# Block sums of a symmetrised matrix in four instructions, and the held groups' stores on SyncE

## The chip, the core and the metric

The kernel runs on one core of a Trainium2 chip. The metric is the device time of one execution in microseconds (us), lower being better; a time given for a kernel is the median over several runs. The profile is of one execution. The engines are TensorE (PE, with its weight loads as PEld), VectorE (DVE), ScalarE (ACT), GpSimd (POOL) and SyncE (SP); SP, ACT and POOL issue the DMA transfers.

## The reference

```python
def reference(x, adj, L0_gnn_W):          # x (8, 4096, 256), adj (4096, 4096), W (256, 256), float32
    HW = jnp.einsum('bnf,fo->bno', x, W)
    A_norm = jax.nn.relu((adj + adj.T) * 0.5)
    D = jnp.sum(A_norm, axis=1)
    d_inv_sqrt = jnp.where(D > 0, jnp.where(D > 0, D, 1.0) ** (-0.5), 0.0)
    DAD = d_inv_sqrt[:, None] * A_norm * d_inv_sqrt[None, :]
    out = relu(jnp.einsum('nm,bmo->bno', jnp.eye(4096) - DAD, HW))
    return _layernorm(x + out, axis=-1)
```

`adj` is sparse, and denser in its first rows and columns: entry (i, j) is set with a probability that falls with i and j.

## The kernel before

The work has two phases. The **first phase** (to about 595 us of the profile) goes over the upper triangle of `adj` in blocks of 512 x 512: row `i` from 0 to 7, column `j` from `i` to 7. For a pair of blocks (i, j) and (j, i) it loads both (`load_adj`, L411, by SyncE, four buffers), transposes one with TensorE in 16 pieces (`symmetrise`, L421), adds the other from SBUF with VectorE, 512 columns at a time (L425), and so makes two blocks `sym` (three buffers). `keep` then applies ReLU and the factor 0.5 with ScalarE (L429), sums every 64 columns into `part` with VectorE (L430), and stores the block to `a_dram` by a DMA that ScalarE issues (L436). The four transposed strips of a block need one PSUM bank each; four banks (`b0`) turn round between these, the transposes of x and the products with W, so TensorE can go on only as VectorE and ScalarE empty them.

Beside the blocks TensorE makes the products with W, one group of 128 rows (all eight batches) at a time (`form`): it transposes x (L519), ScalarE copies the result (L520), TensorE multiplies by W (L530). The result `g` has to be scaled by the row's degree root `r`. For rows whose degrees are known ScalarE scales it out of PSUM (L540) and stores it to `g_dram` (L545). The last ten groups, 22 to 31, are made early and **held** in SBUF (L542). When a row `i` of blocks is through, `degrees(i)` sums `part` (L447), makes `e` (L449), takes the root with GpSimd (L450) and its negative (L451). `release` then scales the held groups of that row, the odd ones with VectorE (L553), the even ones with ScalarE (L555), and stores them to `g_dram` (L556). `lower_diagonal` corrects the diagonal blocks (L459, stored by L462). Groups 22 and 23 belong to row 5, groups 24 to 27 to row 6, groups 28 to 31 to row 7. After its store each group is multiplied with a strip of A (`multiply`, L488, into the banks `lead`), which makes the first 128 rows of the output.

From row 2 on VectorE also builds lists of which pieces of A are not empty (`patterns`, `place`, `place_rest`, `spread`, `index`, L199 to L384), from the sums in `part`.

The **second phase** gathers those pieces of A and the rows of g by indirect DMAs that GpSimd issues (L806, L819; 12 buffers for g), multiplies them (L1008), and finishes each 128 rows with ReLU, residual and layer norm on ScalarE and VectorE; SyncE stores the output (L729). The gathers read `g_dram`, so the first one waits for the last held group's store.

The instructions of an engine run in the order of its list. A scheduler makes that list from the program and from its own costs of instructions, so an edit can move other instructions; pools of buffers and semaphores do the rest. A DMA waits on its issuing engine for what it stores, and everything behind it on that engine waits with it.

Of the kernel before, what the change touches and what calls it, by code (L numbers as in the profile page):

```python
# [11 lines left out]
ALU = mybir.AluOpType  # L12
AX = mybir.AxisListType
# [46 lines left out]
def kernel(  # L60
# [25 lines left out]
    nc = tc.nc  # L86
    B, N, F = x.shape
    FO = w.shape[1]
    P = 128
    S = 512  # L90
    A = S // P
# [5 lines left out]
    Q = 64  # L97
# [17 lines left out]
    part = const.tile([P, NB, N // Q], F32, name="part")  # L115
# [8 lines left out]
    g_dram = dram.tile([N + 1, G], F32, name="g_dram")  # L124
# [270 lines left out]
    with (  # L395
# [31 lines left out]

        def keep(i, j, sym, diag):
            nc.scalar.activation(sym, sym, AF.Relu, scale=0.5)  # L429
            nc.vector.tensor_reduce(  # L430
                part[:, i * A : (i + 1) * A, j * S // Q : (j + 1) * S // Q],
                sym.rearrange("p a (c q) -> p a c q", q=Q),
                AX.X,
                ALU.add,
            )
            nc.scalar.dma_start(  # L436
                a_dram[i * S : (i + 1) * S, j * S : (j + 1) * S].rearrange("(a p) s -> p a s", p=P), sym
            )
            if i == j:
                for a in range(A):  # L440
                    nc.gpsimd.tensor_copy(diag[:, a, :], sym[:, a, a * P : (a + 1) * P])
# [38 lines left out]
        def fetch(m):  # L480

            t = strips.tile([P, P], F32, tag="strip", name=f"strip_{m}")
            load(t, a_dram[m * P : (m + 1) * P, :P])
            return t
# [65 lines left out]
        def release(m):  # L550
            g = held.pop(m)
            if m % 2:
                nc.vector.tensor_scalar(g, g, r[:, m : m + 1], None, ALU.mult)  # L553
            else:
                nc.scalar.mul(g, g, r[:, m : m + 1])  # L555
            nc.scalar.dma_start(g_dram[m * P : (m + 1) * P, :], g)  # L556
            waiting.append((m, g, fetch(m)))

        diags = {}
# [1 line left out]
        def release_all(i):  # L561
            for m in range(i * A, (i + 1) * A):
                if m in held:
                    release(m)
            lower_diagonal(i, diags.pop(i))
# [43 lines left out]
        for i in range(NS):  # L609
            diag = stat1.tile([P, A, P], F32, tag="diag", name=f"diag_{i}")  # L610
            for j in range(i, NS):
# [27 lines left out]
                for (rows, cols, _, _), sym in parts:  # L639
                    keep(rows, cols, sym, diag)  # L640
# [448 lines left out]
```

## Time and profile before

| | us |
|---|---|
| median of 6 runs (1526.8 to 1532.9) | 1530.88 |
| the profiled execution | 1528.14 |
| its span, first to last instruction | 1526.4 |

| engine | busy us | share of the span |
|---|---|---|
| PE | 1443.0 | 95% |
| PEld | 761.8 | 50% |
| DVE | 980.7 | 64% |
| ACT | 371.0 | 24% |
| POOL | 696.0 | 46% |

The groups that the diff touches: 64 sums L430 of 128x2048 elements, 145.5 us busy in all, 2280 ns each; ten stores L556 of 1024 KB, 9.5 us from issue to landing.

How to read it: lines of the timeline give the start and the length in us, engine, line and operation, and in brackets the idle time of the engine just before and what ended it. `L430` is line 430 of the kernel before; a tile's name stands as output<-input. A duration is that of one instruction from its start to its end; instructions that are queued on VectorE overlap a little, so the distance of their starts is shorter. The granted clock is 1.00 when TensorE runs at full speed. In the chain that ended last, each piece of time is put down to the instruction or transfer on which the next one waited.

### The profile page before, as it was taken

How to read it: one execution, taken by the hardware profiler on the slowest of the kernel's cores; microseconds unless marked ns; L12 is line 12 of the kernel's file. 1: busy time of each engine (PE TensorE's matmuls, PEld its weight loads, DVE VectorE, ACT ScalarE, POOL GpSimd, SP SyncE). 2: the span in 40 equal slices, each digit the busy share in tenths (PEclk: the TensorE clock that was granted, in tenths of full speed). 3: DMA queues.
4: the chain of work that ended last, by engine and by line, in shares of the span. 5: the costliest groups of instructions: out<-in, count | busy, mean ns of one | idle time of the engine just before them, and what ended most of it. 6: DMA issues, size and time to landing. Idle time of an engine off the chain costs nothing.

```text
span 1526.4 us, 19342 instructions
## 1 busy us (share of the span) xinstructions
PE 1443.0 (95%) x6440; PEld 761.8 (50%) x6440; DVE 980.7 (64%) x3013; ACT 371.0 (24%) x462; POOL 696.0 (46%) x1053
## 2 busy tenths in 40 slices
PE   5999989989989989999999999999999999999994
PEld 5877877767767764433333333333433333333331
DVE  4676578888646460464759669768046877898533
ACT  3655544535434450010100100100010011001111
POOL 3002010010303315766767666666655767666653
PEclk9999999989999999999999999999999999999997
DMA  9999999999979988999999999999989999999995
GB/s 334 370 371 401 395 380 361 360 369 349 344 250 363 335 345 354 419 417 409 381 398 389 384 408 370 401 389 383 394 306 398 345 388 404 401 396 371 381 397 183
DMA packets 216714, 564.50 MB, mean 370 GB/s; under 512 B 16550, under 2 KB 104918, under 8 KB 180134
## 3 DMA queue, kind: packets, MB, share of 16 engines
q0 software_dynamic: 54224, 304.94, 50.3%
q1 hardware_dynamic: 90352, 123.74, 23.3%
q10 hardware_dynamic: 72032, 134.51, 23.3%
q8 instruction: 54, 0.88, 0.2%
q14 instruction: 52, 0.43, 0.1%
HBM read 443.61 MB, written 136.34 MB: 380 GB/s over the span
## 4 chain that ended last, share of the span: by engine, by line
PE 69%; DMA 14%; DVE 9%; issue 5%; ACT 2%; POOL 2%; POOLq 0%; ACTq 0%; DVEq 0%
PE py L1008 48%; PE pg L530 9%; DMA g<-g_dram,gi 9%; PE lead L488 5%; DMA a_dram<-sym 3%; DVE sym L425 3%; PE xtr L519 3%; PE tr L421 3%; DVE part L430 2%; ACT sym L429 1%; DMA xin<-in_x_dram 1%; PE lists L356 1%; DMA ga<-a_dram,ai 1%; POOL limit L165 0%; POOL base L166 0%
## 5 line engine op out<-in xcount | busy, mean ns | idle before, releaser
L1008 PE MATMUL py<-g,ga 128*64 128x512 f32 (+1 forms) x2872 | 811.9, 597 | 14.7 <-DMA g<-g_dram,gi 12.3
L1008 PEld LDWEIGHTS py<-g,ga 128*64 128x64 f32 (+1 forms) x2872 | 290.9, 150 | 522.3 <-issue 498.6
L819 POOL DMA_INDIRECT g<-g_dram,gi x268 | 307.2, 1146 | 210.9 <-DMA g<-g_dram,gi 82.0
L806 POOL DMA_INDIRECT ga<-a_dram,ai x268 | 291.1, 1086 | 107.5 <-issue 68.3
L681 ACT ACTIVATE y<-py,minus_r 128x512 f32<-128x512 f32 x120 | 82.4, 687 | 806.4 <-PE py L1008 714.1
L692 DVE TENSOR_TENSOR xr<-xr,y 128x2048 f32<-128x2048 f32 x31 | 71.1, 2292 | 303.7 <-ACT y L681 249.3
L530 PE MATMUL pg<-w_sb,xt 128*128 128x256 f32 x1024 | 232.9, 386 | 5.2 <-ACT xt L520 5.2
L425 DVE TENSOR_TENSOR sym<-tr,adj 128x512 f32<-128x512 f32 x256 | 162.8, 683 | 95.6 <-PE tr L421 78.7
L530 PEld LDWEIGHTS pg<-w_sb,xt 128*128 128x128 f32 x1024 | 196.4, 195 | 33.4 <-ACT xt L520 5.6
L430 DVE TENSOR_REDUCE part<-sym 128x32 f32<-128x2048 f32 x64 | 145.5, 2280 | 61.7 <-ACT sym L429 61.7
L421 PE MATMUL tr<-ident,adj 128*128 128x128 f32 x1024 | 138.4, 285 | 31.6 <-DVE sym L425 20.0
L429 ACT ACTIVATE sym<-sym 128x2048 f32<-128x2048 f32 x64 | 122.6, 1916 | 130.9 <-DVE sym L425 118.4
L450 POOL TENSOR_TENSOR r<-e,neg_half 128x4 f32<-128x4 f32 x8 | 8.3, 1039 | 317.0 <-DVE e L449 234.7
L421 PEld LDWEIGHTS tr<-ident,adj 128*128 128x128 f32 x1024 | 118.8, 146 | 61.3 <-DVE sym L425 32.7
L697 DVE BATCH_NORM_STATS2 stats<-xr 128x6 f32<-128x256 f32 x256 | 87.2, 412 | 16.1 <-POOL xr L692 14.9
L519 PE MATMUL xtr<-ident,xin 128*128 128x128 f32 x512 | 72.4, 288 | 16.4 <-DVE sym L425 15.0
L721 DVE TENSOR_SCALAR xr<-xr,mv,root 128x256 f32<-128x256 f32 x248 | 83.6, 409 | 0.1
L488 PE MATMUL lead<-gt,strip 128*128 128x512 f32 x176 | 83.0, 598 | 0.0
L540 ACT ACTIVATE gt<-pg,r 128x512 f32<-128x512 f32 x88 | 60.6, 688 | 75.8 <-PE pg L530 71.9
L520 ACT COPY xt<-xtr 128x512 f32<-128x512 f32 x128 | 67.7, 591 | 45.7 <-PE xtr L519 45.1
L1008 PE MATMUL py<-g_hub,ga 128*128 128x512 f32 x176 | 78.3, 598 | 0.0
L335 DVE TENSOR_TENSOR hot<-iota_q,at 128x1024 bf16<-128x1024 f32 x64 | 74.3, 1221 | 2.8 <-DMA a_dram<-sym 2.8
(139 smaller groups left out, 812.2 us busy)
## 6 DMA issues: line engine op xcount, KB each, us to landing
adj<-in_adj_dram SPq DMA_DIRECT2D x64, 1024.0 KB, 10.6
a_dram<-sym ACTq DMA_DIRECT2D x64, 1024.0 KB, 9.3
xr<-in_x_dram ACTq DMA_DIRECT2D x32, 1024.0 KB, 26.3
out_dram<-xr SPq DMA_DIRECT2D x31, 1024.0 KB, 25.4
xin<-in_x_dram SPq DMA_DIRECT2D x44, 512.0 KB, 11.4
g_dram<-gt ACTq DMA_DIRECT2D x22, 1024.0 KB, 7.6
xin<-in_x_dram POOLq DMA_DIRECT2D x20, 512.0 KB, 7.2
g_dram<-held ACTq DMA_DIRECT2D x10, 1024.0 KB, 9.5
```

What stands on the lines that cost most here:

```text
L421: ins = nc.tensor.transpose(pt[:, c * P : (c + 1) * P], tji[:, c, a * P : (a + 1) * P], ident)
L425: nc.vector.tensor_add(sym[:, a, :], pt, tij[:, a, :])
L429: nc.scalar.activation(sym, sym, AF.Relu, scale=0.5)
L430: nc.vector.tensor_reduce(part[:, i * A : (i + 1) * A, j * S // Q : (j + 1) * S // Q], sym.rearrange("p a (c q) -> p a c q", q=Q), AX.X, A ...
L488: nc.tensor.matmul(lead[c], lhsT=strip, rhs=g[:, c * S : (c + 1) * S], start=not done, stop=len(done) == NB - 1, skip_group_check=True,)
L519: nc.tensor.transpose(pt[:, k, c, :], xin[b // H][:, b % H + k, c * P : (c + 1) * P], ident)
L530: ins = nc.tensor.matmul(pg[:, k * FO : (k + 1) * FO], lhsT=xt[:, b + k, c, :], rhs=w_sb[:, c, :], start=(c == 0), stop=(c == FC - 1),)
L697: nc.vector.bn_stats(stats[:, b, :], z[:, b, :])
L721: nc.vector.tensor_scalar(z[:, b, :], z[:, b, :], mv[:, b, 0:1], rstd[:, b : b + 1], ALU.subtract, ALU.mult,)
L806: nc.gpsimd.indirect_dma_start(out=at if both else at[:, :P], out_offset=None, in_=a_pairs if both else a_rows, in_offset=bass.IndirectOff ...
L819: nc.gpsimd.indirect_dma_start(out=gt, out_offset=None, in_=g_dram, in_offset=bass.IndirectOffsetOnAxis(ap=gi[:, t : t + 1], axis=0), boun ...
L1008: last_product = nc.tensor.matmul(py[2 * u + 1 + b][c][rows, :], lhsT=at[:, off + rows.start : off + rows.stop], rhs=gt[:, c * S : (c + 1) ...
```

## The change

The sums of 64 columns in `keep` are made by one instruction for each of the four 128-row parts of a block, not by one for the whole block: 256 instructions over 512 elements a partition in place of 64 over 2048. The stores of the ten held groups in `release` are issued by SyncE, not by ScalarE. On SyncE's list the stores of groups 22 and 23 stand ahead of the load of the last block (7, 7), and the other eight behind it, ahead of the first store of the output.

```diff
         def keep(i, j, sym, diag):
             nc.scalar.activation(sym, sym, AF.Relu, scale=0.5)
-            nc.vector.tensor_reduce(
-                part[:, i * A : (i + 1) * A, j * S // Q : (j + 1) * S // Q],
-                sym.rearrange("p a (c q) -> p a c q", q=Q),
-                AX.X,
-                ALU.add,
-            )
+
+            for a in range(A):
+                nc.vector.tensor_reduce(
+                    part[:, i * A + a, j * S // Q : (j + 1) * S // Q],
+                    sym[:, a].rearrange("p (c q) -> p c q", q=Q),
+                    AX.X,
+                    ALU.add,
+                )
             nc.scalar.dma_start(
                 a_dram[i * S : (i + 1) * S, j * S : (j + 1) * S].rearrange("(a p) s -> p a s", p=P), sym
             )
...
-            nc.scalar.dma_start(g_dram[m * P : (m + 1) * P, :], g)
+            nc.sync.dma_start(g_dram[m * P : (m + 1) * P, :], g)
             waiting.append((m, g, fetch(m)))
```

## The prediction

> **What bounds the kernel now.** I read the page first, then busy time by stage, then the chain of work that ended last, then the timelines of VectorE, TensorE and ScalarE where that chain leaves TensorE.
>
> ```profile
> span 1526.4 us, 19342 instructions
> PE 1443.0 (95%) x6440; PEld 761.8 (50%) x6440; DVE 980.7 (64%) x3013; ACT 371.0 (24%) x462; POOL 696.0 (46%) x1053
> ```
>
> TensorE is busy for 95% of the span, but both edits lie in the first 570 us. The stages differ (columns: length, then busy us and instructions of PE, PEld, DVE, ACT, POOL, the granted TensorE clock, the DMA share, GB/s):
>
> ```profile
> 40.00:220.00 180.00, 175.27 (x1018) 145.41 (x1018) 115.16 (x135) 101.71 (x128) 14.12 (x26) 1.00 1.04 382
> 220.00:360.00 140.00, 125.35 (x677) 97.59 (x676) 123.53 (x369) 63.13 (x73) 6.00 (x14) 0.95 0.99 360
> 360.00:560.00 200.00, 181.24 (x978) 141.25 (x977) 115.92 (x169) 94.25 (x109) 44.64 (x74) 0.95 0.88 327
> ```
>
> Up to 220 us the DMA engines are full (1.04). From 220 to 360 VectorE is busy 88%, and 98% from 240 to 280, since the index lists are placed there; TensorE loses 15 us. From 360 to 560 TensorE loses 19 us in gaps with single causes. From 564 on the chain is TensorE without a gap until 962, so what the first phase loses is carried to the end.
>
> **The price of one smaller sum.** The rows are the sum over a block and, nearest in size, the sum of 256 columns for the degrees.
>
> ```profile
> L430 DVE TENSOR_REDUCE part<-sym 128x32 f32<-128x2048 f32 x64 | 145.5, 2280 | 61.7 <-ACT sym L429 61.7
> L447 DVE TENSOR_REDUCE deg<-part 128x4 f32<-128x256 f32 x8 | 3.3, 417 | 0.1
> ```
>
> From start to start, with work queued behind, the large one takes 2.19 us (548.66 to 550.85) and the small one 0.32 (546.40 to 546.72). That is 1.04 ns an element and 0.05 us fixed, so 512 elements take 0.59 us; the 512-column adds of L425 follow each other at 0.60. Four make 2.39 us: 0.20 more per block, 64 x 0.20 = 12.8 us of VectorE in all. The bounds: nothing at all, or +0.45 if each shows the 0.68 us that an add lasts by itself minus a little overlap (4 x 0.66 = 2.64). I take 0.20, since the queued rows are the nearest.
>
> The Trainium skill, "VectorE: DVE Perf Modes", section on the TRN2 errata, speaks against this half: each instruction pays a fixed cost, so many small ones pay it many times. Its measured form for a single operation, (N+151)/0.96 ns, would give 4 x 0.69 - 2.29 = 0.47 a block, an estimate of 30 us in all; the queued starts 0.60 apart in this trace show that most of that fixed part overlaps.
>
> **Where 0.20 us reaches the end.** In 40 to 220 the chain contains five sums, but it also goes through stores of 11 us on full DMA engines: I take nothing, and 1.0 if that cover fails. Elsewhere the chain lists the sums in its own pieces:
> - 220 to 300: five, +1.0 us.
> - 320 to 360: four, +0.8.
> - The pair at 378.44, with TensorE idle 2.58 us for the add behind it: +0.4.
> - 448.0, 454.4 and 458.8: +0.6.
> - 515.08, in front of the degrees of row 5, whose root scales the group that TensorE waits 1.04 us for: +0.2.
>
> Together +3.0.
>
> **Two places where the order of VectorE changes.** The changed kernel's list of VectorE instructions is the old one, with quarters of sums slipped between small operations. Two of the moves matter. First, the diagonal block of row 3:
>
> ```profile
> 302.52 0.69 DVE L425 TENSOR_TENSOR sym<-tr,adj 128x512 f32<-128x512 f32 x1
> 303.12 0.17 DVE L326 CAST at<-digit 128x32 f32<-128x32 int32 x1
> 303.21 4.47 DVE L430 TENSOR_REDUCE part<-sym 128x32 f32<-128x2048 f32 x2
> ...
> 308.91 0.69 DVE L425 TENSOR_TENSOR sym<-tr,adj 128x512 f32<-128x512 f32 x1
> 310.08 0.17 DVE L451 TENSOR_SCALAR minus_r<-r 128x4 f32<-128x4 f32 x1 [0.48 <-POOL r L450]
> ...
> 310.36 1.21 DVE L459 SCALAR_TENSOR_TENSOR diag<-ident,minus_e,diag 128x128 f32<-128x128 f32 x4
> ```
> ```profile
> 308.91 1.97 PE L519 MATMUL xtr<-ident,xin 128*128 128x128 f32 x8 [4.99 <-DVE sym L425]
> 310.67 8.06 PE L530 MATMUL pg<-w_sb,xt 128*128 128x256 f32 x32
> ```
>
> Now the second add stands ahead of the pair of sums, the third and fourth behind it; TensorE waits 4.99 us for the PSUM banks they free. In the new list only the first add is ahead; the second and third come after the pair, and the fourth after `minus_r`, which waits for GpSimd's root, and the four L459. With the row's own steps: first add done 302.4, eight sums of 0.6 and a cast to 307.4, degrees and small ones 0.6, add 308.6, the next 309.35, the root 1.04 us after `e` so `minus_r` at 310.0, then 1.85 us of L459 and others, and the fourth add ends at 312.45 instead of 309.5. The last four transposes need its bank and take some 0.6 us, so L530 starts near 313.05 instead of 310.67: **+2.4 us**, with the pair's 0.4 in it.
>
> Second, the end of row 6, where the other edit lies too:
>
> ```profile
> 548.08 0.07 DVE e L449
> ...
> 551.02 1.20 DVE held L553
> ...
> 552.24 0.34 ACTq L556
> ...
> 553.11 2.01 ACT held L555
> ...
> 555.14 0.33 ACTq L556
> ...
> 555.51 0.59 ACT xt L520
> 556.10 0.04 issue
> 556.14 8.24 PE pg L530 x24
> 564.38 30.90 PE lead L488 x72
> ```
>
> TensorE stands idle 5.19 us before 556.14 for the copies L520, which queue on ScalarE behind two scalings L555 and four stores L556. The store of an odd group makes ScalarE wait for VectorE's scaling (552.22), and each issue takes 0.33 to 0.39 us. With the stores on SyncE the two scalings follow directly: 549.31 + 2 x 2.0 = 553.3 instead of 555.51, **-2.2**. But in the new list `e` of row 6 stands behind the four sums of the second block, not ahead: +0.20 for the first block's sums and +2.39 for those. The root and the first L555 move from 549.31 to 551.90, the copies to 555.9: **+0.4** net against 555.51.
>
> The Trainium skill, "DMA: Bandwidth & Descriptors", section "Issuing engines are not separate DMA queues", says that another issuing engine saves only the issue time. By it the gain at this place would be the 1.06 us of three issues, and the net +1.5; the chain shows the wait behind VectorE as well, so I keep 2.2.
>
> On SyncE the ten stores pass one load: the stores of groups 22 and 23 stand ahead of the load of block (7,7). That load could go at 527 (its buffer is freed by the adds that end at 527.2) and is first used at 544.96, after a landing of 10.9 us: 7 us of cover, and the stores are ready at 521.4. Price 0; if a store were stuck past 534, each us costs one. After that nothing stands behind them before the first output. The indirect loads wait for the last store (582.71) and TensorE needs the first at 595.28, with 7 us to land: 5 us of cover, and ScalarE no longer loses its 1.83 us of issue before the last scaling, so the cover grows. Price 0.
>
> **Sum.** 3.0 + 2.4 + 0.4 = 5.8. I take back 0.6: around 263 the new list puts an add ahead of a sum where TensorE idles 0.84 and 0.38 us, and in 220 to 300 full DMA engines hide a little. So +5.2: the profiled execution goes from 1528.14 (span 1526.4 and 1.74 around it) to 1533.3. That execution lies 2.7 us under the median of 1530.88, so the median goes to 1536.
>
> **Rivals.** About 0.2%, or 3.1 us, is what a measurement of this kernel can tell from no change.
> 1. *Covered.* DMA engines at 0.99 to 1.04 up to 360 us hide the sums there, and only 378 to 556 (+1.6) is left with part of the diagonal: 0 to +3, about 1532.5. For: the DMA share. Against: TensorE idles for VectorE in just those stretches.
> 2. *The freed ScalarE wins (faster).* Place: 549 to 556. Price: -2.2 for the gap, and the granted clock, 0.50 from 556 to 562, stays up: 24 matmuls of L530 in 5.18 us, as in the other groups, not 8.24: -3.1. With +2.4 at row 3 and the other sums hidden this gives -2.9, or 1528. It decides if the first L555 of row 6 still starts within 1 us of ScalarE's being free, which the late `e` speaks against.
> 3. *Dearer.* At +0.45 a sum the 15 listed ones cost 6.8, the diagonal 2.9 and row 6 0.9, in all 10.6; with one more spell of half clock (1.0 to 3.1 us, as after the gaps of 4.99 and 5.19) about +12: 1543. Against it: starts 0.60 apart.
>
> **Chances.** Forecast 0.52 (+3 to +8, a tenth of it under 3.1), covered 0.20 (nearly all within 0.2%), freed ScalarE 0.13, dearer 0.15. Faster 0.13, the same 0.20, slower 0.67. The range runs from the middle of the second rival to the dearer case: 1528 to 1543.
>
> **What would show it.** The group of sums: 256, at 0.68 us each, 0.60 apart. VectorE's total up by about 13 us (or more, as single durations overlap). A gap of TensorE near 303 that reaches into 312; ScalarE's two L555 at row 6 back to back, but later; L530 there not earlier than before on the shifted time; from then on the same second phase, shifted. It is wrong if the gap before that L530 closes to 3 us, if the sums start 0.55 or less apart, or if the stretch from 220 to 360 does not grow.

## Result, and the profile after

The changed kernel takes 1536.17 us (median of 20 runs, 1529.99 to 1540.74) against 1530.72 (median of 41) for the kernel before: a ratio of 1.0031, 95% interval 1.002 to 1.0043, or +4.7 us (3.1 to 6.6). A later comparison on one chip gave 1.0020 (1.0004 to 1.0037), or +3.1 us (0.6 to 5.7). So it is slower, by 3 to 5 us as the two centres have it. The profiled execution took 1534.51 us, with a span of 1532.7.

The page's totals after:

```profile
span 1532.7 us, 19533 instructions
PE 1447.2 (94%) x6440; PEld 767.2 (50%) x6440; DVE 992.6 (65%) x3205; ACT 371.7 (24%) x462; POOL 693.1 (45%) x1053
```

VectorE has 192 instructions and 11.9 us more, or 0.186 us for each of the 64 blocks. TensorE's 4 us more are the same 6440 matmuls, with a mean granted clock of 0.980, not 0.984. The group of sums, and the stores, now on SyncE's queue:

```profile
L432 DVE TENSOR_REDUCE part<-sym 128x8 f32<-128x512 f32 x256 | 159.4, 678 | 56.7 <-ACT sym L429 56.7
...
g_dram<-held SPq DMA_DIRECT2D x10, 1024.0 KB, 9.6
```

The three stages of the prediction, with the same columns:

```profile
40.00:220.00 180.00, 173.58 (x1009) 144.15 (x1008) 117.89 (x203) 100.35 (x126) 11.82 (x22) 1.00 1.03 375
220.00:360.00 140.00, 126.16 (x666) 99.16 (x666) 122.56 (x410) 65.50 (x75) 8.30 (x19) 0.94 0.98 355
360.00:560.00 200.00, 181.47 (x997) 141.14 (x995) 121.75 (x235) 88.68 (x103) 39.72 (x67) 0.97 0.87 323
```

These windows stand at fixed times and say little about a shift: after does 11 matmuls fewer in 220 to 360 and 19 more in 360 to 560. I therefore follow landmarks: the starts of L429, ScalarE's 64 rectifications, one for each block.

**Row 3.** VectorE around the diagonal block (lines between those shown are left out), then TensorE:

```profile
306.73 0.69 DVE L425 TENSOR_TENSOR sym<-tr,adj 128x512 f32<-128x512 f32 x1
...
308.10 4.24 DVE L432 TENSOR_REDUCE part<-sym 128x8 f32<-128x512 f32 x7
...
312.83 0.68 DVE L425 TENSOR_TENSOR sym<-tr,adj 128x512 f32<-128x512 f32 x1
...
313.57 0.68 DVE L425 TENSOR_TENSOR sym<-tr,adj 128x512 f32<-128x512 f32 x1
...
316.36 0.69 DVE L425 TENSOR_TENSOR sym<-tr,adj 128x512 f32<-128x512 f32 x1
```
```profile
307.48 0.66 PE L521 MATMUL xtr<-ident,xin 128*128 128x128 f32 x4
313.56 2.82 PE L521 MATMUL xtr<-ident,xin 128*128 128x128 f32 x12 [5.43 <-DVE sym L425]
316.18 8.10 PE L532 MATMUL pg<-w_sb,xt 128*128 128x256 f32 x32
```

The order is the foreseen one: one add ahead of the eight sums, two after them, the fourth behind the small work. But TensorE waits 5.43 us, not 4.99 and 2.4 more. The wait ends with the second add (312.83 + 0.68), and the last transposes have begun when L532 starts at 316.18, before the fourth add begins at 316.36. What the last four do wait for has changed: in the trace before, each group of four waits for VectorE; after, the last group waits for ScalarE. By the turn of the four banks that is the copy of the first four transposes, long done:

```profile
308.89 0.58 ACT L522 COPY xt<-xtr 128x512 f32<-128x512 f32 x1 [0.44 <-ACT sym L429]
```

**Row 6.** The chain of work that ended last (start, us, what):

```profile
557.52 1.05 POOL r L452
558.57 0.02 issue
558.60 3.90 ACT held L557 x2
562.49 0.48 ACT xt L522
562.97 0.04 issue
563.01 7.13 PE pg L532 x24
570.15 30.90 PE lead L490 x72
```

The two scalings stand back to back and no issue lies between them, but the root that they wait for comes late. That is what the prediction describes. How much it is worth needs a fixed point, the last L429 ahead of the root, before and after:

```profile
543.73 1.91 ACT L429 ACTIVATE sym<-sym 128x2048 f32<-128x2048 f32 x1 [0.47 <-DVE sym L425]
```
```profile
550.52 1.91 ACT L429 ACTIVATE sym<-sym 128x2048 f32<-128x2048 f32 x1 [0.52 <-DVE sym L425]
```

TensorE's 24 matmuls come 12.41 us behind it before and 12.49 after. TensorE's own timeline after:

```profile
558.09 1.99 PE L532 MATMUL pg<-w_sb,xt 128*128 128x256 f32 x8 [1.95 <-DVE sym L425]
563.01 7.13 PE L532 MATMUL pg<-w_sb,xt 128*128 128x256 f32 x24 [2.93 <-ACT xt L522]
```

The gap right before the 24 matmuls is 2.93 us, under the 3 us that the prediction named as a sign that it is wrong. But it has only been split: another 1.95 us now stand before the eight matmuls ahead of them, 4.88 in all against 5.19, and the start behind the landmark has not moved.

### The profile page after: what moved, and what is told of

Read it like the earlier page. It is cut to its first block, busy times and chain, and to the rows that moved or that the text cites. A ratio compares the mean times of both kernels' runs of the same rounds, so it can differ in the third digit from the quotient of the medians.

```text
span 1532.7 us, 19533 instructions
## 1 busy us (share of the span) xinstructions
PE 1447.2 (94%) x6440; PEld 767.2 (50%) x6440; DVE 992.6 (65%) x3205; ACT 371.7 (24%) x462; POOL 693.1 (45%) x1053
## 4 chain that ended last, share of the span: by engine, by line
PE 67%; DMA 15%; DVE 7%; issue 6%; ACT 2%; POOL 2%; POOLq 0%; DVEq 0%
PE py L1010 48%; PE pg L532 8%; DMA g<-g_dram,gi 8%; DMA a_dram<-sym 5%; PE lead L490 4%; PE xtr L521 3%; DVE part L432 2%; PE tr L421 2%; DVE sym L425 2%; DMA xin<-in_x_dram 1%; ACT sym L429 1%; DMA ga<-a_dram,ai 1%; PE lists L356 1%; ACT xt L522 0%; POOL strip L480 0%
## 5 line engine op out<-in xcount | busy, mean ns | idle before, releaser
L821 POOL DMA_INDIRECT g<-g_dram,gi x268 | 302.5, 1129 | 206.9 <-DMA g<-g_dram,gi 75.8
L808 POOL DMA_INDIRECT ga<-a_dram,ai x268 | 295.1, 1101 | 111.0 <-issue 68.5
L532 PE MATMUL pg<-w_sb,xt 128*128 128x256 f32 x1024 | 233.2, 386 | 4.9 <-ACT xt L522 2.9
L532 PEld LDWEIGHTS pg<-w_sb,xt 128*128 128x128 f32 x1024 | 196.8, 195 | 33.4 <-ACT xt L522 3.3
L432 DVE TENSOR_REDUCE part<-sym 128x8 f32<-128x512 f32 x256 | 159.4, 678 | 56.7 <-ACT sym L429 56.7
L421 PE MATMUL tr<-ident,adj 128*128 128x128 f32 x1024 | 138.7, 286 | 32.8 <-DVE sym L425 19.4
L429 ACT ACTIVATE sym<-sym 128x2048 f32<-128x2048 f32 x64 | 122.6, 1915 | 138.2 <-DVE sym L425 125.7
L421 PEld LDWEIGHTS tr<-ident,adj 128*128 128x128 f32 x1024 | 119.0, 146 | 61.9 <-DVE sym L425 32.8
L521 PE MATMUL xtr<-ident,xin 128*128 128x128 f32 x512 | 74.6, 295 | 18.2 <-DVE sym L425 16.7
L521 PEld LDWEIGHTS xtr<-ident,xin 128*128 128x128 f32 x512 | 61.8, 150 | 34.5 <-DVE sym L425 26.6
```

The source lines that it names most:

```text
L421: ins = nc.tensor.transpose(pt[:, c * P : (c + 1) * P], tji[:, c, a * P : (a + 1) * P], ident)
L432: nc.vector.tensor_reduce(part[:, i * A + a, j * S // Q : (j + 1) * S // Q], sym[:, a].rearrange("p (c q) -> p c q", q=Q), AX.X, ALU.add,)
L521: nc.tensor.transpose(pt[:, k, c, :], xin[b // H][:, b % H + k, c * P : (c + 1) * P], ident)
L532: ins = nc.tensor.matmul(pg[:, k * FO : (k + 1) * FO], lhsT=xt[:, b + k, c, :], rhs=w_sb[:, c, :], start=(c == 0), stop=(c == FC - 1),)
L808: nc.gpsimd.indirect_dma_start(out=at if both else at[:, :P], out_offset=None, in_=a_pairs if both else a_rows, in_offset=bass.IndirectOff ...
L821: nc.gpsimd.indirect_dma_start(out=gt, out_offset=None, in_=g_dram, in_offset=bass.IndirectOffsetOnAxis(ap=gi[:, t : t + 1], axis=0), boun ...
```

## Experiments

All ran on one core, and each ratio is against the kernel before on the same chip; intervals are of 95%. Line numbers shift with the edits: L430/L432 are the sums, L555/L557 ScalarE's scalings and L530/L532 the matmuls into `pg`.

**The two halves.** Theory: the sums cost, and the stores pay only once the sums are split. Rival: each half stands for itself.

```diff
# sums alone
-            nc.vector.tensor_reduce(part[...], sym.rearrange("p a (c q) -> p a c q", q=Q), AX.X, ALU.add)
+            for a in range(A):
+                nc.vector.tensor_reduce(part[...], sym[:, a].rearrange("p (c q) -> p c q", q=Q), AX.X, ALU.add)
# stores alone
-            nc.scalar.dma_start(g_dram[m * P : (m + 1) * P, :], g)
+            nc.sync.dma_start(g_dram[m * P : (m + 1) * P, :], g)
```

> Only the sums are split in four; the held groups' stores stay on ScalarE. Here, too, the root's input e of row 6 stands behind the four sums of the second block. Theory of the prediction: ScalarE still queues its stores there, so the copies of x come 2.2 us later than in the changed kernel: 1538 (+7 to +8 against before). Rival (ScalarE's stores cost nothing, the sums are everything): the same as the changed kernel, 1536 (+5).

Measured: 1533.35 us against 1529.94, ratio 1.0021 (1.0006 to 1.0036). Slower, by 3.2 us (0.9 to 5.5) and not by 7; the rival's +5 lies inside the interval.

> Only the held groups' stores go to SyncE; the sums stay whole. In this list, too, e of row 6 stands behind the whole sum of the second block. Theory of the prediction: -2.2 for the freed ScalarE and +2.2 for the late e, so no change (1530 to 1532). Rival (the freed ScalarE wins): the gap ahead of L530 near 556 closes to 3 us and the clock stays up, 1526 (-5).

Measured: 1531.23 us, ratio 1.0009 (0.9993 to 1.0026): no change that can be seen. The chain at row 6, sums alone and then stores alone:

```profile
559.07 2.01 ACT held L557
561.08 0.02 issue
561.10 0.34 ACTq L558
561.44 0.05 issue
561.49 2.01 ACT held L557
...
564.68 6.89 PE pg L532 x24
```
```profile
556.56 3.90 ACT held L555 x2
560.46 0.48 ACT xt L520
560.93 0.04 issue
560.98 8.38 PE pg L530 x24
```

With whole sums and SyncE's stores the scalings are back to back too, but `e` and the root stand behind the second block's whole sum, and the gain is used up.

**The halves once more, with the kernel before and the whole change beside them on one chip.** I wanted this because the profiles of the first set disagreed by 3 us long before row 3. (In the first of these texts the clock times of the landmark are wrong: it is the 16th L429, at 122.39 us in the first profile of before and at 126.0 in that of the changed kernel.)

> The kernel before, once more, on the chip that also runs the two halves and the whole of the change. It should time 0.0% against itself. If most of the +3.6 us that the profile of the changed kernel showed at 122 us is the clock of the first 60 us and not the sums, this second profile of the kernel before has a granted clock under 1.00 somewhere in its first 60 us, and stands 2 to 3 us later at 122 us than its first profile (118.5 us against 122 us of the same landmark). The rival, that the sums cost it, expects the second profile within 0.5 us of the first there.

Measured: 1532.25 us against 1533.39 for the same program, ratio 0.9988 (0.9967 to 1.0009). In its profile the granted clock is 1.00 all through the first 60 us, so that part of the theory fails here; yet it stands 1.80 us later at the landmark. The rival fails too.

> Sums in four instructions, stores still on ScalarE, beside the other three of the square. Theory: +3 to +4 us on the kernel before, all of it from the sums at row boundaries.

Measured: ratio 1.0024 (1.0011 to 1.0038), +3.7 us.

> Stores on SyncE alone, whole sums. Theory: no change, -0.5 to +1 us, since row 6 gains nothing.

Measured: ratio 1.0012 (0.9988 to 1.0036): unclear, and wider than the effect.

> The whole change. If the parts add as the traces of row 6 have it (the stores save 1.2 to 1.7 us once the sums are split), it is +2 to +3 us on the kernel before and under the sums alone by 1 to 2 us; if the saving in row 6 is given back in the second phase, it equals the sums alone within 1 us, at +3 to +5 us.

Measured: ratio 1.0020 (1.0004 to 1.0037), +3.1 us. Times cannot separate the whole change from the sums alone. The traces can, place by place. Row 3 is the time from the first L519 to the first L530; row 6 runs from the last L429 before the root to the 24 matmuls. Each cell has the first and the second profile (L521 and L532 where the sums are split):

| us | before | stores alone | sums alone | both |
|---|---|---|---|---|
| row 3 | 8.09, 8.09 | 8.09, 8.09 | 8.70, 8.70 | 8.70, 8.70 |
| row 6 | 12.41, 12.41 | 12.14, 12.14 | 13.74, 13.74 | 12.49, 12.50 |
| row 6, to the end of the 24 matmuls | 20.65, 20.10 | 20.52, 17.58 | 20.63, 20.88 | 19.63, 19.64 |
| 28th L429, against 216.77 | 0, +2.05 | +3.93, -0.21 | +3.80, +1.22 | +3.52, +2.85 |
| from there to the 63rd L429, growth | 0, -0.26 | +1.18, +0.32 | +3.41, +2.17 | +3.27, +0.90 |

The first two lines repeat to 0.01 us. The stores save 0.27 with whole sums and 1.25 with split ones: inside the 1.2 to 1.7 expected here, not the 2.2 expected of the sums alone. The third line does not repeat, since the 24 matmuls themselves took from 5.45 to 8.38 us in two executions of the stores alone, with the granted clock; up to their end the whole change is 0.5 to 1.0 us shorter than before. The last two lines swing by up to 4 us between executions of one program, so a single profile could not have settled them.

**Sums of 128 columns, sixteen to a block.** This multiplies the suspected cost.

```diff
+            for a in range(A):
+                for c in range(4):
+                    nc.vector.tensor_reduce(part[two columns], sym[:, a, 2 * c * Q : 2 * (c + 1) * Q]..., AX.X, ALU.add)
```

> Each block's sums in sixteen instructions of 128 columns, stores on ScalarE: the suspected cost made large. At 0.20 us from start to start that is 3.2 us a block, +1.0 instead of +0.2, so 64 us more of VectorE. Theory (only some 15 to 17 sums between 220 and 556 lie on the path): +15 to +19. Rival (the first 220 us pay as well, 14 to 18 sums more): +30 to +36.

Measured: 1552.72 us (median of 5) against 1534.77, ratio 1.0096 (1.0063 to 1.0128), or +14.7 us (9.7 to 19.6): the theory's number fits, the rival's does not. The order of VectorE's list moves here too, so this is not the instructions' own cost alone. From the page, and VectorE's timeline:

```profile
L432 DVE TENSOR_REDUCE part<-sym 128x2 f32<-128x128 f32 x1024 | 209.4, 281 | 55.5 <-ACT sym L429 55.4
```
```profile
91.76 3.18 DVE L432 TENSOR_REDUCE part<-sym 128x2 f32<-128x128 f32 x16 [3.57 <-ACT sym L429]
94.86 4.86 DVE L425 TENSOR_TENSOR sym<-tr,adj 128x512 f32<-128x512 f32 x8
```

Sixteen sums take 3.10 us to the next instruction, 0.91 more than the 2.19 of one. At the 28th L429, 27 of them or 24.6 us of VectorE lie behind; the landmark stands at +5.41, where six profiles with whole sums have 1.92 on average (-0.21 to 3.93). So about 3.5 of 24.6 us are paid in the first 217 us (1.5 to 5.6 by that spread). From there to the 64th L429, 36 more (32.8 us) cost 17.45 us. In this one profile the cover is good in front and half open behind.

**The same, in the first row and column only.**

```diff
+            if i == 0 or j == 0:   # sixteen sums
+            else:                  # one sum, as before
```

> Sixteen instructions per block only in row 0 and column 0 of the blocks (15 blocks, 15 us more of VectorE in the first 125 us), stores on ScalarE, the rest as before. Theory of the prediction (full DMA engines hide them): 0 to +1. Rival (each step of the row waits for its sum): +1.0 for each of 8 steps, +8, up to +15.

Measured: ratio 1.0038 (1.0009 to 1.0068), +5.8 us by the times, while the profile's span is 1532.9. Its landmark at 217 us is +4.75, 2.8 above the mean of the whole-sum profiles, for 15.9 us more of VectorE. By the 63rd L429 it stands at +1.57, no later than the four profiles with whole sums in the old places (0 to 5.11, 1.75 on average), so in this profile the delay is made up. The times (+1.4 to +10.4) exclude the theory's 0 to +1 by little, and the upper part of the rival; profile and times do not agree, and the size stays open.

**Four sums in the first row and column only; two sums to a block everywhere.**

```diff
# first row and column
+            if i == 0 or j == 0:   # four sums, else one
# two to a block
+            for a in range(0, A, 2):
+                nc.vector.tensor_reduce(part[two rows], sym[:, a : a + 2]..., AX.X, ALU.add)
```

> The sums are split in four only in the first row of blocks, that is for the 15 blocks of row 0 and column 0, all in the first 120 us; the order of the other instructions is that of before. Theory of the prediction (full DMA engines hide the sums there): no change, 0 to +0.5. Rival (every step of the row waits for its sum, DMA engines full or not): 7 to 8 sums of 0.20 on the path, +1.5, and up to +3.6 if the difference of the two traces at 120 us is all due to the sums and not to the clock's start.

> Two instructions of 1024 columns per block instead of four of 512, stores on ScalarE. VectorE pays 0.06 more per block, a third. The order at row 3 is moved as in the changed kernel, the one at row 6 is not. Theory of the prediction: a third of 3.0 plus 2.0 for the move at row 3, +3. Rival (only the instructions' own time counts, moves do not): a third of the whole, +1.5 to +2.

Measured: 1.0007 (0.9989 to 1.0025) and 1.0004 (0.9987 to 1.0022). In microseconds that is -1.7 to +3.8 and -2.0 to +3.4, and both intervals hold the theory and the rival. Their profiles carry disturbances of several us (+9 at 167 us in the first), so they decide nothing on the total. At row 3, though, the run with two sums to a block shows something. It puts the adds in the same new order, and here TensorE's matmuls into `pg` do wait for the fourth add (VectorE, then TensorE):

```profile
316.41 0.69 DVE L425 TENSOR_TENSOR sym<-tr,adj 128x512 f32<-128x512 f32 x1
```
```profile
313.62 2.82 PE L520 MATMUL xtr<-ident,xin 128*128 128x128 f32 x12 [5.19 <-DVE sym L425]
317.15 1.22 PE L531 MATMUL pg<-w_sb,xt 128*128 128x256 f32 x2 [0.71 <-DVE sym L425]
```

Row 3 takes 9.38 us, 1.29 more than before and 0.68 more than with sums in four; 2.0 were expected.

**The root of row 6 put first.** Whole sums, SyncE's stores, and the sum of block (7, 6) issued behind the degrees of row 6, so that `e` does not stand behind it.

```diff
+            if (i, j) == (NS - 1, NS - 2):
+                put_off.append(sums)      # issued after degrees(i)
+            else:
+                sums()
...
-            nc.scalar.dma_start(g_dram[m * P : (m + 1) * P, :], g)
+            nc.sync.dma_start(g_dram[m * P : (m + 1) * P, :], g)
```

> Whole sums, stores on SyncE, and the sum of the second block of row 6 is written after the degrees, so that e of row 6 stands ahead of it as before. Theory: the freed ScalarE now brings its 2.2 us, and up to 1 us of clock: -2 to -3 against before (1528). Rival (stores on ScalarE cost nothing): 0.

```profile
550.50 3.90 ACT held L563 x2
554.39 1.44 ACT xt L528 x3
```

The copies start 9.42 us behind the last L429 (544.97), against 11.78 before: -2.4 us, as expected, and the 24 matmuls run in 5.45 us. That last number is no proof of the freed ScalarE: the second profile of the stores alone, where the copies come late, has it as well.

```profile
555.98 5.45 PE L530 MATMUL pg<-w_sb,xt 128*128 128x256 f32 x24 [1.24 <-ACT xt L520]
```

At the end of the span the ratio is 0.9985 (0.9961 to 1.001), or -2.3 us (-6.0 to +1.5): it holds the theory's -2 to -3 and no change alike.

**The second blocks' sums and the index patterns also behind the diagonal block's adds, in rows 1 to 6.**

```diff
+            if i == NS - 1 and 0 < j < NS - 1:
+                put_off.append(sums)      # issued after the next block's last add
...
-                    patterns(u)
+                    put_off.append(lambda u=u: patterns(u))
```

> Whole sums, stores on SyncE; at the end of rows 1 to 6 the sum of the second block, and the list patterns that read it, stand behind the four adds of the next row's diagonal block instead of ahead. Theory (TensorE's gaps at 303, 384 and 556 are VectorE's order): the first two close by 2.2 us each, with clock 1 us each, and the last by 2.2, so -5 to -9 (1522 to 1526). Rival (a sum put off is paid later): -2.

Measured: 1535.3 us against 1534.77, ratio 1.0001 (0.9975 to 1.0026), or -3.8 to +4.0 us: the theory's -5 to -9 is excluded, the rival's -2 is not. At row 3 the gap does close: from the first transposes to the first matmul into `pg` it takes 2.52 us (307.73 to 310.25), not 8.09. The chain shows that TensorE gets through the first phase 2.8 us earlier than before (592.45 against 595.28):

```profile
554.41 7.13 PE pg L538 x24
561.55 30.90 PE lead L496 x72
592.45 26.02 PE py L1019 x79
```

But the first indirect load of `g` is later, not earlier. GpSimd's timeline:

```profile
583.25 1.05 POOL L817 DMA_INDIRECT ga<-a_dram,ai  x1 [7.15 <-DMA g_dram<-held]
584.61 1.06 POOL L830 DMA_INDIRECT g<-g_dram,gi  x1 [0.31 <-issue]
```

It starts at 584.61, against 582.71 before, although the last store of a held group was issued at 566.5 and not at 570.9. GpSimd's wait for those stores ended at 583.25, no sooner than before, with a DMA share of 1.02 from 560 to 575 us (1.03 before). TensorE's 80th matmul into `py` then comes 26.4 us behind the first, against 24.4 before, so 2.0 of the 2.8 us are lost by there. Whether the remainder reaches the end cannot be told from these times.

## Why the prediction was right, and where its sum was not

**Direction and total: right.** 1536.0 was forecast and 1536.17 measured; the second comparison, at +3.1 us, would have put it at about 1534. The terms were not all of the right size, and the close agreement is partly luck: the larger ones were too large, and one that was put at nothing likely was not.

**The price of a sum: right.** 0.20 us a block was taken; VectorE's total gives 0.186, and four sums take 2.37 us to the next instruction (20.14 to 22.51), where 2.39 was worked out. The Trainium skill, "VectorE: DVE Perf Modes", section on the TRN2 errata, has a fixed cost for each instruction; by its form the estimate was 30 us of VectorE in all, and the trace has 11.9. For single durations the form, which the page gives for an add, comes close for these sums too: by estimate 291 ns for 128 columns, against 281 here, and 691 ns for 512, against 678. Queued, sixteen short sums follow each other at 0.19 us, so most of the fixed part overlaps.

**Row 3: the order right, the wait wrong, the size four times too large.** +2.4 was forecast; from transposes to L532 it is +0.61 in all four profiles with sums in four. The step that failed is "the last four transposes need its bank". They did not wait for the fourth add, which began after them; they waited for ScalarE, whose copy had been done since 309.47. What the new order costs is the wait grown from 4.99 to 5.43 (0.44) and four of the transposes moved behind it, where the granted clock is 0.50 (0.17). The gap that was to reach into 312 ends, counted from the first transposes, where 308.7 was before. With sums in two the next matmuls did need that bank, and row 3 cost 1.29: which bank a tile gets is part of the new order, and the prediction carried over the old one.

**Row 6: the net right, the share of the stores not.** The root's scaling comes 8.08 us behind the L429 against 5.58 (+2.5; +2.59 was forecast), and the start of the 24 matmuls is +0.1 (+0.2 for the copies) where +0.4 was forecast. From the first scaling to the copies it is 6.20 us before, 4.97 with the sums alone and 3.89 with both: -2.3 in all, but only 1.08 of it is the stores'. The rest goes already with the sums alone, since VectorE's scalings then follow the root at once and ScalarE no longer waits for them behind a sum. With the root in its old place the stores are worth the whole 2.4. The Trainium skill, "DMA: Bandwidth & Descriptors", section "Issuing engines are not separate DMA queues", allows only the issue time, 1.06 us here. The runs have 0.27, 1.25 and 2.4, depending on where the root stands: in the changed kernel the gain is near that issue time, and with the root in its old place it is more than twice as much. There the trace before has ScalarE behind an issue that waits until 552.22 for VectorE's scaling, and that wait goes too.

**The sums between: about right.** 3.0 less 0.6 was forecast. The growth from 217 us to the 63rd L429 is 2.1 us with the whole change (3.27 and 0.90), against 0 and -0.26 before; without row 3's 0.6 this leaves 1.5, with an uncertainty of about 1. The page's stretch from 220 to 360, which the prediction wanted to see grow, does so in one profile by landmarks (+1.68 from the 28th to the 43rd L429) and not in the other (+0.11); before has 0 and +0.87. That test was too fine for one profile.

**Cover in the first 220 us: held in part.** Nothing was taken, and 1.0 if it fails. The first profile of after shows +3.5 there, but stores alone, with whole sums, shows +3.9 once and -0.2 once. By the profile of the sixteen sums, 14% of what is added is paid: 27 x 0.186 x 0.14 = 0.7 us, an estimate. The four profiles with sums in four stand 2.85 us late on average at the 28th L429, 0.9 above the six with whole sums; the spread is too wide to tell that from nothing. The times of the sixteen sums in row 0 alone, +1.4 to +10.4, speak for more. So the term put at nothing was likely some tenths to 1 us, and its size is not settled.

Added up: 0.7 + 1.5 + 0.6 + 0.1 = 2.9 us, and the times say 3.1 and 4.7. Counted to the end of row 6's matmuls it would be 0.5 to 1.0 less. What lies between sum and times is not resolved.

**"What the first phase loses is carried to the end": right for losses, not shown for gains.** The sixteen sums carried 14.7 us to the end. The 2.4 and 2.8 us won in the last two experiments lie inside the noise of their times (-6.0 to +1.5 and -3.8 to +4.0). Their profiles show where part of it went: the first loads of `g` came no earlier, and by the 80th matmul into `py` TensorE had lost 1.5 and 2.0 us. The prediction's 5 us of cover for those loads is a narrow bound in that direction.

**The rivals.** *Covered* (0 to +3, about +1.6) is just excluded by the first comparison (at least +3.1) and not by the second (at least +0.6); by the profiles the cover holds in part in the first 220 us and less behind. *Freed ScalarE* needed a root within 1 us, and the root came 2.5 us late; its -2.2 does appear in the run with the root first (-2.4 at the gap). Its other part, the 24 matmuls at the full clock, came there and also once in the stores alone, so it is not shown to follow from ScalarE. *Dearer* is excluded by the 0.186 and by the times (at most +6.6).

## What to carry to other kernels

Before an engine is freed, look at what its next instruction waits for: here ScalarE's 2.2 us were worth 0.27 to 1.25 while the root stood behind more than 2 us of sums in VectorE's order. When a buffer's release is moved, find the last release that the reader really needs in the new order: with sums in four the fourth add was late and nobody waited for it, with sums in two the next matmuls did, for 0.71 us. Measure a place from a landmark just ahead of it: up to the start of row 6's 24 matmuls that repeats to 0.01 us, against some us for absolute times; their own length does not.

## What was unexpected of the hardware

Executions of one program do not begin alike. Stores alone, first and second profile (on two chips), by 20 us (the granted clock is the third number from the end):

```profile
0.00:20.00 20.00, 7.83 (x37) 7.63 (x38) 6.24 (x22) 3.19 (x2) 14.07 (x376) 0.85 0.84 293
20.00:40.00 20.00, 16.43 (x99) 14.39 (x98) 13.74 (x16) 10.15 (x12) 0.35 (x2) 0.93 1.02 375
40.00:60.00 20.00, 18.72 (x109) 16.07 (x108) 11.84 (x12) 11.01 (x15) 0.00 (x0) 0.97 1.01 335
```
```profile
0.00:20.00 20.00, 8.16 (x43) 7.79 (x44) 6.53 (x23) 3.44 (x3) 14.20 (x377) 1.00 0.85 298
20.00:40.00 20.00, 16.11 (x102) 13.24 (x101) 14.04 (x16) 10.64 (x14) 0.23 (x1) 1.00 1.04 382
40.00:60.00 20.00, 19.41 (x111) 16.47 (x110) 11.08 (x11) 11.91 (x16) 0.00 (x0) 1.00 1.02 353
```

At 122 us they stand 3.3 us apart (+3.09 and -0.25), the slower being the one with the lower clock. It is not the chip alone: the whole change, on the second chip too, began at 0.87, 0.93 and 0.95 and was 2.92 us late there. Nor is it the clock alone: the second profile of before had 1.00 throughout and was 1.8 us late. The second phase varies as well: from the first indirect load of `g` to the end of the span, sums alone took 943.0 us once (1533.8 - 590.76) and 949.2 once (1536.2 - 586.98).
